# Moving an image's closing pass one image later

## The chip, the cores and the metric

The kernel runs on one core of a Trainium2 chip. The metric is the time of one execution on the device, in microseconds, lower is better; the runs of one kernel are told by their median. The engines are TensorE (PE in the profile; PEld is its weight load), VectorE (DVE), ScalarE (ACT), GpSimd (POOL) and SyncE (SP), which here only issues transfers.

## What is computed

Four images of 96 channels and 128 x 128 pixels pass two layers. Layer 0 is a state-space block; here only its end matters, a norm over channels and a projection whose result, added to the input, is `xnew`. Layer 1 splits the normed image into a positive and a negative half, convolves them, and combines:

```python
xr, x1, x2 = _relu_split_norm(x, sc1, sc2, res_coef, nc1, nc2)
y1 = _layer_norm(_attn_conv(x1, x2, aw1, aw2, aw3))      # od in the kernel
y2 = _layer_norm(_conv2d(x2, w_conv2, K // 2)) * x1      # c2d in the kernel
y = jnp.concatenate([y1, y2], axis=1)
return xr + _conv2d(y, w_full, 0) + b_full[None, :, None, None]
```

`_attn_conv` makes three maps of an image (key, query and value), a softmax over products of the first two, and convolves the value with that softmax as its weights. Both layer norms run over a whole image, so their means and variances exist only when the last row of the image is done. The last line is therefore a pass of its own over the image: the close.

## The kernel before

Up to about 3640 us the scan of layer 0 runs, and beside its end the maps of image 0. What follows is a loop over images `b` (L2598). For each image a foreground, `attention(img, at)` (L1959), works through eleven strips of 12 rows (the last has 8). For images 1 to 3 it makes the maps first: for each strip key and value from `x1p` (m = 0), query and the second convolution from `x2p` (m = 1), on TensorE with weights `wd`, combined on VectorE (`outputs`, L1531). After the last strip stands the softmax (`taps.weights()`, L1683), then the stack of weights `wa` is loaded (`product_stack`, L1367), and the same eleven strips are convolved with them: here called the products. Image 0 has its maps already (`img.mapped`) and only has products here.

The statistics are gathered on the way: `bn_stats` of the second convolution into `c2a` and `c2b`, of the products into `ost` (L2106). Those buffers exist twice, for even and for odd images.

Beside the foreground runs a background, the generator `light`, a chain of:

- `norm` (`ssm_output`, L936): the norm and projection of the next image, mostly on TensorE, which writes `xnew`;
- `split` (`split_norm`): reads `xnew` twice, first for counts, then for the halves `x1p` and `x2p`, with `L1267` on VectorE once for every half plane (64 in an image) and the planes from it on VectorE and GpSimd;
- `close` (`attn_output`, L2299): first the set-up, in which `own_weights` (L2259) and `c2_weights` (L2224) aggregate the statistics (`bn_aggr` at L192 and L2235) and make two weight matrices `w1` and `w2`; then 16 pieces of 1024 pixels. A piece loads `od`, `c2d` and `xnew`, makes `x1` (L2283, L2284), `c2` (L2326) and the residual `e` (L2288 to L2290), multiplies on TensorE (L2334, L2335), adds (L2337 for image 0, L2339 for the others) and stores to `out` (L2341).

`co_run` (L302) interleaves the two at recording: each step of the foreground yields a cost, and the background is advanced by as much. `drain` (L359) records all that is left. Since norm and split of image `b + 1` stand ahead of the close of image `b - 1` in the chain, and `drain(light)` (L2603) stands at the head of images 2 and 3, close 0 is recorded in one piece at the head of image 2, and close 1 beside the products of image 2 with its end at the head of image 3. Image 3 has close 2 (with `share` 2, which counts each piece double and so spreads it), then `before` (L2359), which stores `x1` and `e` of the last image, and after the maps `beside`, which combines the second convolution. What is left of the last image comes after the loop (`after`, L2418).

After recording, a scheduler places the instructions on each engine's queue. It need not keep the recorded order between foreground and background; transfers are issued mostly from SP's queue, in order too.

Of the kernel before, what the change touches and what calls it, by code (L numbers as in the profile page):

```python
# [9 lines left out]
F32 = mybir.dt.float32  # L10
# [7 lines left out]
C = 96  # L18
H = W = 128
L = H * W  # L20
# [51 lines left out]
def kernel(  # L72
# [26 lines left out]
    nc = tc.nc  # L99
# [87 lines left out]
    def combine(ps, stats, mat, name, mv=None):  # L187


        if mv is None:  # L190
            mv = small.tile([stats.shape[0], 2], F32, name="mv", tag=f"mv{stats.shape[0]}")
            nc.vector.bn_aggr(mv, stats)  # L192
        n = mv.shape[0]
        p1 = bank(ps)[:n, 0:2]
        nc.tensor.matmul(p1, lhsT=mat, rhs=mv, start=True, stop=True)  # L195
        r = small.tile([n, 2], F32, name=name, tag=name)
        nc.vector.tensor_copy(r, p1)
        d2 = small.tile([n, 1], F32, name=f"d2{n}", tag=f"d2{n}")
        nc.vector.tensor_sub(d2, mv[:, 0:1], r[:, 0:1])
        nc.vector.tensor_mul(d2, d2, d2)  # L200
        p2 = bank(ps)[:n, 0:2]
        nc.tensor.matmul(p2[:, 0:1], lhsT=mat, rhs=d2, start=True, stop=True)  # L202
        nc.vector.tensor_add(r[:, 1:2], r[:, 1:2], p2[:, 0:1])
        return r, mv
# [154 lines left out]
    def drain(gen):  # L359
        for _ in gen:  # L360
            pass
# [1005 lines left out]
    def product_stack(pool, wd, name, eng=nc.sync):  # L1367


        n = wd.shape[3]  # L1370
        w1 = pool.tile([128, NP, n], F32, name=f"{name}1", tag=f"{name}1")
        w2 = pool.tile([128, NP, n], F32, name=f"{name}2", tag=f"{name}2")
        w3 = pool.tile([128, 2, n], F32, name=f"{name}3", tag=f"{name}3")
        eng.dma_start(w1[0:96], wd[:, 0])
        eng.dma_start(w1[96:128], wd[64:96, 1])
        for h in (1, 2):
            eng.dma_start(w2[64 * h - 64 : 64 * h], wd[0:64, h])
        for j, of in enumerate((FOUR, TWO)):
            for i, p in of:
                eng.dma_start(w3[p : p + 32, j], wd[64:96, 2, i])  # L1380
        return w1, w2, w3
# [577 lines left out]
    def attention(img, at):  # L1959
# [9 lines left out]
        if not img.mapped:  # L1969
# [62 lines left out]
            for s, (r0, r) in enumerate(chunks):  # L2032
# [56 lines left out]
                        yield from taps.some(1 if m else 2)  # L2089
                taps.complete(s, min(r, 3 * NV - r0))  # L2090
            yield from taps.weights()
            ws = product_stack(p1, taps.wt, "wa", nc.scalar)
            img.maps_made()
        else:
            ws = product_stack(p1, img.watd, "wa", nc.scalar)
        yield 3.0
        for i, (r0, r) in enumerate(chunks):
            t, fill, load = at.strip()
            oc = own[0:C, : AR * W]
            here = img.last and r0 >= H - OWN  # L2100
            if here:
                oc = img.last.own[0:C, (r0 - H + OWN) * W :]

            def out(oc=oc, r0=r0, r=r, here=here):
                for a in range(0, r, 4):
                    nc.vector.bn_stats(  # L2106
                        img.ost[:, (r0 + a) // 4], oc[:, a * W : (a + 4) * W]
                    )
                if not here:
                    nc.sync.dma_start(img.od[:, r0 * W : (r0 + r) * W], oc[:, : r * W])  # L2110
                img.finished = r0 + r == H

            v = oc[:, : r * W]
            if img.mapped:
                v = v.rearrange("p (h w) -> p h w", w=W)
            else:
                v = v.rearrange("p (h j t) -> p h j t", j=TW, t=TN)
            to = [(0, C, v)]
            evac = outputs(p2, C, r * TN, to, later, out)
            yield from products(ps, [(0, C, 0, t, 0, r)], ws, later, evac, fill=[  # L2120
                both(fill[0], load[0]), fill[1], both(fill[2], load[1]),
                fill[3], both(fill[4], load[2]), fill[5],
            ])
# [97 lines left out]
            yield from lift(H)  # L2221
            later.flush()

    def c2_weights(img, ps, pool):  # L2224


        n = NSTRIP
        mva, mvb = (pool.tile([128, 2], F32, name=f"mv_{i}") for i in "ab")
        for mv, st, p, e, k in (
            (mva, img.c2a, 96, 128, 4 * n - img.mapped),  # L2230
            (mvb, img.c2b, 0, 64, 2 * n - (not img.mapped)),
            (mvb, img.c2b, 64, 128, 2 * n - 1),
        ):
            v = st[p:e, :k].rearrange("p c s -> p (c s)")
            nc.vector.bn_aggr(mv[p:e], v)  # L2235
        halves = ((mva[96:128], m96[96:128]), (mvb, mrows[img.mapped]))

        def over(n):
            pt = bank(ps)[:, 0:n]
            for i, (mv, mat) in enumerate(halves):  # L2240
                nc.tensor.matmul(
                    pt, lhsT=mat, rhs=mv[:, 0:n], start=(i == 0), stop=(i == 1)
                )
            return pt

        s2 = pool.tile([128, 2], F32, name="s2")
        nc.vector.tensor_copy(s2, over(2))
        for mv, p in ((mva, 96), (mvb, 0)):
            d = mv[p:128, 0:1]
            nc.vector.tensor_sub(d, d, s2[p:128, 0:1])  # L2250
            nc.vector.tensor_mul(d, d, d)
        nc.vector.tensor_add(s2[:, 1:2], s2[:, 1:2], over(1))
        r2 = col("r2")
        rsqrt(r2, s2[0:C, 1:2])
        w2 = pool.tile([C, C], F32, name="w2")
        nc.vector.tensor_scalar(w2, wful[:, 1], r2, None, ALU.mult)
        return s2, w2

    def own_weights(img, ps, pool):  # L2259

        so, _ = combine(ps, img.ost.rearrange("p c s -> p (c s)"), mean96, "so")
        ro = col("ro")
        rsqrt(ro, so[:, 1:2])
        w1 = pool.tile([128, C], F32, name="w1")
        nc.vector.tensor_scalar(w1[0:C], wful[:, 0], ro, None, ALU.mult)
        nso = col("nso")
        nc.vector.tensor_scalar(nso, so[:, 0:1], -1.0, None, ALU.mult)
        pt = bank(ps)[C : C + 1, 0:C]  # L2270
        nc.tensor.matmul(pt, lhsT=img.keep["low"][:, 1:2], rhs=ident, start=True, stop=False)
        nc.tensor.matmul(pt, lhsT=nso, rhs=w1[0:C], start=False, stop=True)  # L2272
        nc.vector.tensor_copy(w1[C : C + 1], pt)
        return w1[0 : C + 1]
# [171 lines left out]
    class Image:  # L2446


        def __init__(self, b):
            self.b = b  # L2450
            self.xnew = dram.tile([C, L], F32, name="xnew", bufs=3)
            self.x1p, self.x2p, self.vp = planes[b % 2]
            self.x1d, self.x2d, self.vd = maps if b == 0 else (None, None, None)
            self.stats = istats[b % 2].tile([C, NCH, 6], F32, name="xstats", tag="xstats")
            self.cnt = istats[b % 2].tile([C, 5, NS], F32, name="cnt", tag="cnt")
            self.keep = {}
            self.mapped, self.lifting = False, False
            self.done = [0, 0]
            self.finished = False
            self.last = None  # L2460
            self.maps_made = lambda: None
            self.watd = None if b else dram.tile([C, 3, NP, C], F32, name="watd", bufs=1)

        def begin(self):

            self.c2d, self.od = (dram.tile([C, L], F32, name=n) for n in ("c2d", "od"))
            n = NSTRIP
            self.c2a, self.c2b, self.ost = (
                istats[self.b % 2].tile([p, k, 6], F32, name=m, tag=m)
                for m, p, k in (("c2a", 128, 4 * n), ("c2b", 128, 2 * n), ("ost", C, H // 4))  # L2470
            )
# [121 lines left out]
    def maps_made(last):  # L2593
        maps_only.close()
        pool = ctx.enter_context(tc.tile_pool(name="e2", bufs=1, side="left"))
        last.kept = pool.tile([C, NS, SN], F32, name="e2")

    for b in range(NB):  # L2598
        after = []
        if b:  # L2600
            if b > 1:
                drain(light)
            imgs[b].begin()  # L2603
            if b + 1 < NB:
                imgs[b + 1] = Image(b + 1)
                after.append(imgs[b + 1].norm(yms[(b + 1) // 2][(b + 1) % 2], psr, "right"))
                after.append(
                    imgs[b + 1].split(psr, "right", lambda i, second: second)
                )
            after.append(imgs[b - 1].close(psr, "right", 1.0 if b + 1 < NB else 2.0))  # L2610
            if b + 1 == NB:
                last = imgs[b].last = LastOutput(imgs[b], psr, "right")
                imgs[b].maps_made = lambda: maps_made(last)
                after += [last.before(), last.beside()]
        light = chain(light, *after)
        left = imgs[b].attend(at)
        co_run(left, light, 1.0 if b else 1.5)
        drain(left)
# [79 lines left out]
```

## Time and profile before

| | us |
|---|---|
| median of 3 runs | 6416.27 |
| lowest, highest | 6413.48, 6428.01 |
| the profiled execution's own time | 6409.68 |
| its span in the profile | 6407.8 |
| mean granted TensorE clock | 0.902 |

| stage (us from the span's start) | foreground | background |
|---|---|---|
| 3826 to 4502 | maps of image 1 | end of split 1, norm 2, split 2 |
| 4502 to 4632 | products of image 1 | end of split 2 |
| 4632 to 5430 | maps of image 2 | close 0, norm 3, split 3 |
| 5430 to 5612 | products of image 2 | most of close 1 |
| 5612 to 6195 | maps of image 3 | end of close 1, close 2, `before` |
| 6195 to 6356 | products of image 3 | `beside` |

The stages of the second table are cut where the first matmul of each stage starts on TensorE; the background is told by the stores of its parts. A row of the profile's view by stretches gives the length of the stretch and then, engine by engine, its busy time and the number of its instructions, the granted clock of TensorE, the mean busy share of the 16 DMA engines and the rate in GB/s. A row of its groups gives the line, the engine, the operation, what it writes and reads, the shapes and the number; then the busy time in us and the mean of one in ns; then the idle time of the engine before them and what ended it. A row of its waits gives who waited for whom, the total in us, the number of times and the longest.

### The profile page before, as it was taken

Reading aid. Unit: us, or ns where it says so; the run is one execution under the profiler, and the core shown is the slowest. Engines: PE = TensorE matmul, PEld = TensorE weight load, DVE = VectorE, ACT = ScalarE, POOL = GpSimd, SP = SyncE. Lnnn points to the kernel's source line nnn. Section 1 sums busy time; section 2 is a strip of 40 time slices with the busy share of each in tenths; the row PEclk is TensorE's granted clock in tenths of the full one; section 3 lists DMA queues with packets and bytes.
Section 4 is the critical chain, followed back from the end, with each engine's and each line's share of the span. In section 5 each row is a group of like instructions: output and inputs, shape, how many; then the busy total and the mean of one; then the engine's idle time right before and its main releaser. Section 6 shows DMA issues by size and latency. Waiting matters only on the chain. (4 is left out here: it accounts for less than half of the span.)

```text
span 6407.8 us, 76468 instructions
## 1 busy us (share of the span) xinstructions
PE 5253.4 (82%) x23264; PEld 2254.8 (35%) x23264; DVE 4699.9 (73%) x7132; ACT 3759.4 (59%) x4770; POOL 3238.6 (51%) x2476
## 2 busy tenths in 40 slices
PE   6889988987888643989988588977888877889888
PEld 2333322322222111444433234345333444345553
DVE  4247878988989768989844686468774687988767
ACT  1247767787787666777622465466644665545642
POOL 1326757978879554979822234436304365022310
PEclk9899989998999765999999799989989888999989
DMA  6766777775675766676667686665776656967668
GB/s 155 175 160 189 198 199 199 214 221 163 198 202 171 202 183 207 196 213 179 182 185 195 166 228 163 195 169 156 214 199 184 175 149 165 245 167 180 191 168 221
DMA packets 897706, 1205.30 MB, mean 188 GB/s; under 512 B 230644, under 2 KB 745642, under 8 KB 884816
## 3 DMA queue, kind: packets, MB, share of 16 engines
q1 hardware_dynamic: 866640, 1145.36, 65.5%
q0 software_dynamic: 16336, 38.51, 2.3%
q10 hardware_dynamic: 14320, 16.54, 0.9%
q8 instruction: 187, 3.06, 0.2%
q14 instruction: 223, 1.83, 0.1%
HBM read 777.82 MB, written 345.62 MB: 175 GB/s over the span
## 5 line engine op out<-in xcount | busy, mean ns | idle before, releaser
L633 PE MATMUL bank<-y,wp 128*128 128x512 f32 (+3 forms) x3584 | 1310.9, 622 | 83.8 <-DMA y<-y 41.0
L866 POOL TENSOR_TENSOR y<-y,dl 128x1024 f32<-128x1024 f32 x384 | 1058.5, 2757 | 263.0 <-DVE dl L858 240.3
L833 POOL TENSOR_TENSOR dl<-dl,u 128x1024 f32<-128x1024 f32 x384 | 1008.8, 2627 | 253.1 <-ACT dA L809 121.1
L854 DVE TENSOR_TENSOR_SCAN dA<-dA,pBC 128x512 f32<-128x512 f32 x768 | 981.6, 1278 | 30.7
L2169 PE MATMUL bank<-y,wn 128*64 128x384 f32 (+5 forms) x2408 | 680.1, 507 | 58.3 <-DMA y<-x1d 34.1
L1477 PE MATMUL two<-ya,wd 128*64 128x192 f32 (+3 forms) x2376 | 582.2, 414 | 174.0 <-ACT odd L1550 65.1
L633 PEld LDWEIGHTS bank<-y,wp 128*128 128x128 f32 (+3 forms) x3584 | 456.2, 168 | 749.3 <-issue 651.1
L858 DVE TENSOR_TENSOR dl<-dA,pBC 128x512 f32<-128x512 f32 x768 | 528.5, 688 | 255.8 <-PE pBC L747 183.8
L747 PE MATMUL pBC<-xr,wbc 60*128 60x512 bf16 (+1 forms) x1536 | 457.8, 404 | 311.5 <-DVE dA L854 239.1
L1938 ACT COPY yb<-ya 64x768 f32<-64x768 f32 (+1 forms) x660 | 537.7, 815 | 195.5 <-PE two L1477 113.8
L676 ACT ACTIVATE dl<-pd,dtb 128x512 f32<-128x512 f32 x768 | 485.5, 684 | 187.9 <-PE pd L747 171.5
L1477 PE MATMUL two<-yb,wd 128*64 128x192 f32 (+3 forms) x2376 | 559.0, 400 | 4.0 <-ACT yb L1938 4.0
L837 DVE TENSOR_TENSOR pBC<-dl,pBC 128x512 f32<-128x512 f32 x768 | 527.5, 687 | 8.8 <-POOL dl L833 7.8
L2169 PEld LDWEIGHTS bank<-y,wn 128*64 128x64 f32 (+3 forms) x2408 | 310.3, 169 | 357.2 <-issue 186.2
L809 ACT ACTIVATE dA<-dl,negA 128x1024 f32<-128x1024 f32 x384 | 420.3, 1141 | 2.3
L1477 PEld LDWEIGHTS two<-ya,wd 128*64 128x64 f32 (+1 forms) x2376 | 262.2, 165 | 370.9 <-ACT odd L1550 75.0
L676 ACT ACT_TABLE_LOAD x248 | 318.2, 1283 | 91.9 <-PE pd L747 79.7
L747 PEld LDWEIGHTS <-wbc 60*128 60x128 bf16 (+1 forms) x1536 | 103.1, 96 | 752.1 <-issue 739.3
L1477 PEld LDWEIGHTS two<-yb,wd 128*64 128x64 f32 (+1 forms) x2376 | 289.7, 167 | 150.5 <-issue 42.1
L1477 PE MATMUL two<-ya,wa 128*96 128x384 f32 (+1 forms) x528 | 231.2, 521 | 72.9 <-DMA ya<-vp 27.0
L1550 ACT COPY odd<-two 128x384 f32<-128x384 f32 (+5 forms) x176 | 115.8, 658 | 291.3 <-PE two L1492 179.1
L1406 POOL TENSOR_TENSOR pl<-x 96x256 f32<-96x256 f32 (+3 forms) x396 | 275.2, 710 | 0.0
(322 smaller groups left out, 9105.4 us busy)
## 6 DMA issues: line engine op xcount, KB each, us to landing
u<-zb SPq DMA_DIRECT2D x192, 1024.0 KB
yms<-y SPq DMA_DIRECT2D x96, 512.0 KB
xn<-xnew SPq DMA_DIRECT2D x128, 384.0 KB
ya<-vp SPq DMA_DIRECT2D x120, 336.0 KB
y<-y SPq DMA_DIRECT2D x128, 258.2 KB
zb<-z SPq DMA_DIRECT2D x64, 512.0 KB
y<-yms SPq DMA_DIRECT2D x64, 512.0 KB
ya<-x1p SPq DMA_DIRECT2D x90, 336.0 KB
```

The source lines that it names most:

```text
L633: nc.tensor.matmul(blocks(pz[p:e]), lhsT=ws[k][:, d, c : c + e - p], rhs=window(ys[k], at, d, n), start=(i == 0), stop=(i == len(terms) - 1),)
L676: nc.scalar.activation(dst, src, AF.Softplus, bias=bias)
L747: nc.tensor.matmul(p, lhsT=w[rows], rhs=xr[rows, at : at + CH], start=True, stop=True)
L809: nc.scalar.activation(live[m]["dA"], live[m]["dl"], AF.Exp, scale=negA[:, g % 3, k : k + 1])
L833: nc.gpsimd.tensor_mul(t, t, u_view(n))
L837: nc.vector.tensor_mul(p, live[n]["dl"][:, bass.ts(half, CH)], p)
L854: nc.vector.tensor_tensor_scan(h, h, p, init, ALU.mult, ALU.add)
L858: nc.vector.tensor_mul(live[n]["dl"][:, sl], live[n]["dA"][:, sl], live[n]["C", half])
L866: nc.gpsimd.tensor_add(v, v, t.rearrange("p (a b) -> p a b", b=W))
L1477: nc.tensor.matmul(of(to[p:e], r), lhsT=w[:, i, c : c + e - p], rhs=tiles(t[k][PAIR[i]][:, SLOT[i]], o, r), start=(k == 0), stop=False,)
L1938: nc.scalar.copy(yb[k][64 * h - 64 : 64 * h, :, :n], ya[k][0:64, :, h * TN : h * TN + n])
L2169: nc.tensor.matmul(pc[p:e, :n].rearrange("p (h w) -> p h w", w=W), lhsT=w[:, c : c + e - p], rhs=v[:, :, 0:W], start=(i == 0), stop=(i == ...
```

## The change

A close runs one image later. Image 1's background is then norm 2 and split 2 alone; image 2's is close 0, norm 3, split 3, with the close first; image 3's is close 1, close 2, `before` and `beside`, all closes with `share` 1. The `drain(light)` at the head of images 2 and 3 is gone.

Since an image's buffers of statistics are written again two images later, a new function `c2_totals` makes means and variances as soon as the image's maps are done, before its product weights are loaded, and `out` does so for `ost` with the last strip. They are kept in `mvs`, six columns in the pool `small`, which keeps two. In DRAM, `xnew` gets a fourth buffer, `c2d` and `od` a third.

```diff
             yield from taps.weights()
+            c2_totals(img)
             ws = product_stack(p1, taps.wt, "wa", nc.scalar)
             img.maps_made()
         else:
+            c2_totals(img)
             ws = product_stack(p1, img.watd, "wa", nc.scalar)
...
-                img.finished = r0 + r == H
+                if r0 + r == H:
+                    nc.vector.bn_aggr(img.mvs[0:C, 4:6], img.ost.rearrange("p c s -> p (c s)"))
+                    img.finished = True
...
-    def c2_weights(img, ps, pool):
+    def c2_totals(img):
         n = NSTRIP
-        mva, mvb = (pool.tile([128, 2], F32, name=f"mv_{i}") for i in "ab")
+        img.mvs = small.tile([128, 6], F32, name="mvs", tag="mvs")
+        mva, mvb = img.mvs[:, 0:2], img.mvs[:, 2:4]
         for mv, st, p, e, k in (
...
             nc.vector.bn_aggr(mv[p:e], v)
+
+    def c2_weights(img, ps, pool):
+        mva, mvb = img.mvs[:, 0:2], img.mvs[:, 2:4]
...
-        so, _ = combine(ps, img.ost.rearrange("p c s -> p (c s)"), mean96, "so")
+        so, _ = combine(ps, None, mean96, "so", img.mvs[0:C, 4:6])
...
-            self.xnew = dram.tile([C, L], F32, name="xnew", bufs=3)
+            self.xnew = dram.tile([C, L], F32, name="xnew", bufs=4)
...
-            self.c2d, self.od = (dram.tile([C, L], F32, name=n) for n in ("c2d", "od"))
+            self.c2d, self.od = (dram.tile([C, L], F32, name=n, bufs=3) for n in ("c2d", "od"))
...
+    closes = {NB - 2: (0,), NB - 1: range(1, NB - 1)}
     for b in range(NB):
         after = []
         if b:
-            if b > 1:
-                drain(light)
             imgs[b].begin()
+            after += [imgs[i].close(psr, "right", 1.0) for i in closes.get(b, ())]
             if b + 1 < NB:
                 imgs[b + 1] = Image(b + 1)
                 after.append(imgs[b + 1].norm(yms[(b + 1) // 2][(b + 1) % 2], psr, "right"))
...
-            after.append(imgs[b - 1].close(psr, "right", 1.0 if b + 1 < NB else 2.0))
```

## Prediction

> **What bounds the kernel now.** I read the page first, then cut the second half of the run into stretches, then asked which instructions fill the stretches that the change touches, then divided the last maps by strip. The page's first part gives averages:
>
> ```profile
> PE 5253.4 (82%) x23264; PEld 2254.8 (35%) x23264; DVE 4699.9 (73%) x7132; ACT 3759.4 (59%) x4770; POOL 3238.6 (51%) x2476
> ```
>
> Two engines stand high and neither is full; the page's chain breaks off after 1% and covers only the last microseconds. So the answer must come by stretch. The stage of image 1 is 3826 to 4632, that of image 2 4632 to 5612, that of image 3 5612 to 6356. The cuts are where strips of maps begin on TensorE (eleven strips of 12 rows to an image).
>
> ```profile
> core 0: us, PE busy (x) PEld busy (x) DVE busy (x) ACT busy (x) POOL busy (x), PEclk, DMA share, GB/s
> 3826.00:3976.00 150.00, 127.27 (x832) 71.19 (x832) 108.66 (x201) 80.35 (x110) 70.08 (x107) 0.91 0.59 156
> 3976.00:4222.00 246.00, 216.38 (x1211) 93.92 (x1212) 120.07 (x265) 112.79 (x159) 100.45 (x132) 0.97 0.67 186
> 4222.00:4502.00 280.00, 211.70 (x1493) 137.20 (x1491) 225.68 (x469) 190.69 (x281) 152.93 (x227) 0.86 0.61 160
> 4502.00:4632.00 130.00, 117.98 (x412) 50.74 (x412) 107.75 (x207) 83.75 (x110) 40.78 (x58) 0.96 0.81 222
> 4632.00:4777.00 145.00, 117.17 (x349) 44.34 (x346) 113.72 (x130) 56.34 (x57) 13.71 (x13) 0.84 0.73 203
> 4777.00:5029.00 252.00, 227.62 (x1251) 95.15 (x1250) 120.49 (x266) 116.82 (x164) 99.26 (x133) 0.96 0.67 188
> 5029.00:5095.00 66.00, 46.20 (x296) 27.88 (x295) 42.92 (x94) 47.73 (x78) 11.45 (x20) 0.82 0.67 171
> 5095.00:5430.00 335.00, 256.87 (x1790) 167.97 (x1788) 278.40 (x555) 200.84 (x284) 205.56 (x295) 0.84 0.58 151
> 5430.00:5612.00 182.00, 164.53 (x502) 67.07 (x502) 153.94 (x198) 93.64 (x109) 5.70 (x16) 0.95 0.90 241
> 5612.00:5916.00 304.00, 273.34 (x1536) 145.30 (x1537) 249.64 (x363) 144.70 (x178) 82.10 (x102) 0.95 0.68 176
> 5916.00:6195.00 279.00, 236.58 (x1779) 154.46 (x1777) 196.67 (x344) 156.97 (x202) 84.24 (x137) 0.92 0.66 179
> 6195.00:6356.00 161.00, 148.72 (x466) 62.08 (x466) 120.86 (x177) 64.82 (x82) 5.41 (x6) 0.93 0.84 219
> ```
>
> In the rows of 3976 and 4777 a norm runs beside maps: TensorE near 90%, VectorE under 50%. In the rows of 4222 and 5095 a split does: VectorE 81 and 83%. The first strip of image 2 (4632 to 4777) holds all of close 0, the products of image 2 (5430 to 5612) hold 13 of the 16 pieces of close 1, and the first five strips of image 3 hold its other 3 and close 2. VectorE is at 78 to 85% there. Compare the two rows of products, 4502 and 5430: the same matmuls take 130 us beside a bit of a split and 182 beside a close.
>
> What a piece of a close (1024 pixels) costs, from VectorE's groups between 4632 and 6356:
>
> ```profile
> L2284 DVE SCALAR_TENSOR_TENSOR x<-xx,kept,x 96x1024 f32<-96x1024 f32 x64 | 84.3, 1317 | 50.4 <-ACT x L2283 34.4 <-DMA od<-own 12.8 <-DMA out<-x 2.7
> L2339 DVE TENSOR_TENSOR x<-bank,e 96x512 f32<-96x512 f32 x64 | 64.8, 1036 | 21.5 <-PE bank L2335 20.9
> L2337 DVE TENSOR_TENSOR x<-bank,e 96x512 f32<-96x512 f32 x32 | 21.5, 683 | 9.9 <-PE bank L2335 9.6
> ```
>
> Four such passes (median 1.275 each, L2284, L2289, L2290, L2326) and two additions: 4 x 1.275 + 2 x 1.036 = 7.2 us of VectorE, for image 0 with L2337 6.5. TensorE has four matmuls, eight records of 0.59 (3.4 us of streaming), ScalarE two passes of 1.23, SP three loads and a store of 393 KB each. What a piece costs in time shows where strips of the last maps carry different numbers. Records of L2334, four to a piece, in strips 1 to 4:
>
> ```profile
> 5679.00:5751.00 72.00, 11.88 (x24) 3.35 (x24) 0.95 0.72 189
> 5751.00:5805.00 54.00, 5.96 (x12) 1.72 (x12) 0.97 0.76 194
> 5805.00:5869.00 64.00, 7.99 (x16) 2.28 (x16) 0.97 0.64 158
> 5869.00:5916.00 47.00, 3.93 (x8) 1.31 (x8) 1.00 0.72 189
> ```
>
> 6, 3, 4 and 2 pieces take 72, 54, 64 and 47 us. The best line is 36 + 6.3 per piece. From two pieces on, a piece costs about its VectorE time. The last two strips, with nothing beside them, take 45 and 56: below two pieces it costs little.
>
> [...] But the change puts closes (VectorE) beside bare maps, not beside the norm, which would have VectorE to spare; the norm keeps its strips to itself. [...] image 2's exponentials end on ScalarE by 5410.2, but VectorE's reciprocal of their sum (L1701) runs at 5414.88, behind the 16 small instructions of close 1's set-up that stand before it. Hence I count what stands ahead of what in the built order.
>
> **The change, part by part.** The profiled execution took 6409.7 us (span 6407.8), 6.6 under the median of 6416.3; the sums are made against the first.
>
> Where things stand comes from the order of the built kernel. Nothing moves up to the end of image 0's direct maps, and image 1's stage is the same but for three aggregates. Image 2: the 16 pieces of close 0 stand in strips 0, 1, 2 (3, 7, 6 on TensorE) instead of all in strip 0; the norm moves from strips 1 to 3 to strips 3 to 5; the split's half-plane instructions (L1267) from strips 5 to 10 to strips 7 to 10, with 20 of 64 from the end of the maps on. Close 1 leaves the products. Image 3: its strips get 0.5, 7, 7, 7, 8, 2.5 pieces, where they had about 4, 6, 3, 4, 2 and none; `before` (L2366) follows behind, as before at four pieces a strip. The products of image 3 and the end keep theirs.
>
> Image 2, maps, now 798 us (4632 to 5430). Strip 0: the burst gives 145 = 41.5 + 16 x 6.5, so 41.5 + 3 x 6.5 = 61. Strips 1 and 2: 36 + 7 x 6 = 78 and 36 + 6 x 6 = 72. The other eight strips carry norm and split just as image 1's last eight do, 246 + 280 = 526; image 2's own norm rows are a little longer, so 530. Sum 741: 57 less. In this is also the softmax without close 1's set-up in front (3 to 4 us).
>
> Image 2, products, now 182. Image 1's took 130 with 15 half-plane instructions; here there are 20, each with its share of the planes about 2.5 us of VectorE, so 12 us on an engine 83% busy. 137: 45 less. DMA, at 0.90 now, falls to the 0.81 of image 1.
>
> Image 3, maps, now 583. Strips 1 to 4, now 237 us, with 7, 7, 7, 8 pieces over the line's 36: at 6.3 each (the line) 327, at 7.2 (VectorE's time) 353. I take 6.7 and 338, so 101 more. Strip 0 loses its pieces of close 1 on TensorE, but VectorE does three ahead: 50 for 67. Strip 5, 2.5 pieces and `before`: 51 for 47. Strips 6 to 10: 4 more for `before` standing one piece later. Sum 92 more. The moved pieces' 13 x 1.57 = 20 MB spread over some 390 us, so DMA goes from 176 to about 190 GB/s, under what the products bear (241).
>
> Image 0's transition (3640 to 3682): the aggregates (L2235, 1.34 and 0.71) now stand before the softmax's maximum, with VectorE without a gap; TensorE waits 27 us here. Three loads of `wa` on ScalarE's queue now stand behind two copies that wait for `vp`. Together 2 to 4 us, against about 1 that the lifted planes win by going ahead: 2 more. At the ends of maps 1 to 3 the aggregate of `c2a` lies in a gap of VectorE, waiting for TensorE (2.4 us at 4478): nothing; without that gap 1.3 each. The aggregate of `ost` only changes its place. The third and fourth DRAM buffers cost no instruction; `mvs` has two buffers, and image 2 wants the first back some 500 us after close 0 has read it. The `drain` removed has nothing left to drain after image 1.
>
> Sum: -57 - 45 + 92 + 2 = -8 us. The change moves VectorE's work and removes none; what it gains is the place where a close costs most (the products, 182 - 137), and it pays nearly as much in the last maps.
>
> **The rivals.** A: the trade above, nearly even: 6408 (own range 6388 to 6428, from 10 us either way in each of the two large sums).
> B, slower: crowded closes cost more than their VectorE time. Place: strips 1 to 4 of image 3, 29 pieces. SP issues in order, and a store that waits for VectorE holds back the `ya` loads behind it; in the stages shown it did so 11 times:
>
> ```profile
> SPq L2341 <- DVE x L2339: 61.9, 11, 9.6
> ```
>
> Also each piece needs the two banks of the piece before. For: VectorE was busy only 78% in the burst and 82% beside close 2. Strips 1 to 4 hold 29 x 7.2 us of closes and 4 x 22 of their own (a bare strip's VectorE rows), 297 us; at 0.80 that is 371, 33 more than I took: +25, 6441. Against: the products had the same chain at 85%. The trade turns negative from 7.0 us a piece, and shows from 7.4.
> C, faster: the pieces cost 6.3, image 2 takes image 1's 526 and 130: -8 - 11 - 4 - 7 = -30, or -45 if the first strips overlap better too: 6371 to 6386. For: VectorE at 45 to 55% in the bare strips. Against: `before` takes those strips.
> D: the change doesn't do what it says, because the scheduler puts the closes back. The built order excludes it.
>
> **How the numbers follow.** A 0.50, B 0.29, C 0.20, D 0.01. I predict A's 6408. The range: A's and C's and B's centres with the ends of the strips' price, 6368 to 6446. A measurement of this kernel can tell about 0.2% (13 us) from no change. A is faster than that in a third of its width and seldom slower; with C faster 0.37, with B slower 0.30, 0.33 between.
>
> **What would show it.** Right: the products of image 2 in 132 to 142 us; image 2's maps in 730 to 755; strips 1 to 4 of image 3 at 80 to 90 each with VectorE at 85% or more, 29 pieces in them; image 1 unchanged in its 806. Wrong: strips at 95 and over, with TensorE waiting for `ya` or L2339 (B); last maps under 650 (C); image 2's products still above 160, which would mean that it was not the close that held them; or a change in image 1's stage, which my account leaves out.

## The result and the profile after

The change makes the kernel slightly slower. Its median is 6428.91 us over 18 runs, that of the kernel before in the same comparison 6413.48 over 18; the ratio is 1.0023, 95% interval 1.0012 to 1.0033, so 8 to 21 us. The prediction said 6408, 8 us less than before. The profiled execution has a span of 6418.8 us and a mean granted clock of 0.899 (0.902 before).

Line numbers after the constructor of the statistics are 9 higher than before: `first_half` is L2292 and L2293, `residual` L2297 to L2299, the close's product and additions L2335, L2343 to L2348, its store L2350, `before`'s load L2375 and stores L2389. The first line of the page, set beside the one shown before:

```profile
PE 5294.5 (82%) x23264; PEld 2269.0 (35%) x23264; DVE 4686.4 (73%) x7132; ACT 3765.8 (59%) x4770; POOL 3232.3 (50%) x2476
```

The same number of instructions, and VectorE's busy time even falls by 13.5 us; TensorE's rises by 41. The view by stretches shows where, cut at the same first matmuls as before (first image 2's norm, its split, its products; then the first five strips of image 3's maps, the other six, its products):

```profile
core 0: us, PE busy (x) PEld busy (x) DVE busy (x) ACT busy (x) POOL busy (x), PEclk, DMA share, GB/s
4817.00:5085.00 268.00, 240.46 (x1241) 99.88 (x1242) 116.29 (x257) 115.16 (x163) 97.63 (x132) 0.92 0.63 174
5085.00:5373.00 288.00, 216.76 (x1504) 139.79 (x1502) 231.34 (x471) 188.00 (x277) 150.02 (x221) 0.85 0.60 157
5373.00:5510.00 137.00, 121.68 (x411) 51.89 (x412) 107.40 (x201) 87.33 (x113) 46.42 (x67) 0.93 0.79 220
5510.00:5893.00 383.00, 339.26 (x1623) 165.84 (x1624) 313.51 (x434) 167.36 (x195) 70.74 (x101) 0.91 0.69 183
5893.00:6211.00 318.00, 264.82 (x1797) 165.31 (x1795) 213.17 (x358) 165.71 (x210) 84.76 (x138) 0.89 0.64 174
```

By stage, from the two traces:

| stage | before | forecast | after |
|---|---|---|---|
| maps of image 1 and its products | 806 | 806 | 809 |
| maps of image 2 | 798 | 741 | 754 |
| products of image 2 | 182 | 137 | 137 |
| maps of image 3 | 583 | 675 | 701 |
| of these, strips 1 to 4 | 237 | 338 | 345 |
| of these, strips 5 to 8 (they hold `before`) | 178 | not told apart | 221 |

The maps of image 1, which of all versions only the very last one touches, took between 669 and 680 us in the 19 other traces; a difference of a few us between two traces shows nothing by itself.

Strips 1 to 4 came out near the forecast, in the records of the matmul L2343 with 7, 7, 7 and 8 pieces:

```profile
5548.00:5621.00 73.00, 13.96 (x28) 3.67 (x28) 1.00 0.69 187
5621.00:5708.00 87.00, 16.49 (x28) 4.73 (x28) 0.91 0.70 187
5708.00:5795.00 87.00, 16.66 (x28) 4.92 (x28) 0.88 0.69 185
5795.00:5893.00 98.00, 18.57 (x32) 5.83 (x32) 0.86 0.66 172
```

They do lose clock from strip to strip (third number from the end: 1.00, 0.91, 0.88, 0.86). The larger surprise lies behind them. Strips 5 to 8 of the kernel before, then of the kernel after:

```profile
5916.00:6094.00 178.00, 155.75 (x1155) 98.75 (x1154) 140.88 (x220) 110.04 (x134) 58.09 (x84) 0.95 0.69 193
```

```profile
5893.00:6113.00 220.00, 184.23 (x1170) 108.63 (x1169) 159.62 (x235) 120.46 (x144) 57.61 (x83) 0.90 0.67 188
```

Nearly the same work (15 matmuls and 15 VectorE instructions more, the last two to three pieces of close 2), 42 us more. No engine is full (TensorE, the busiest, 184 of 220 us); the granted clock is lower, 0.90 for 0.95.

### The profile page after: what moved, and what is told of

Its sections match the earlier page's. It is cut to its first block, busy times and chain, and to the rows that moved or that the text cites. A ratio compares the mean times of both kernels' runs of the same rounds, so it can differ in the third digit from the quotient of the medians.

```text
span 6418.8 us, 76472 instructions
## 1 busy us (share of the span) xinstructions
PE 5294.5 (82%) x23264; PEld 2269.0 (35%) x23264; DVE 4686.4 (73%) x7132; ACT 3765.8 (59%) x4770; POOL 3232.3 (50%) x2476
## 5 line engine op out<-in xcount | busy, mean ns | idle before, releaser
L1477 PE MATMUL two<-ya,wd 128*64 128x192 f32 (+3 forms) x2376 | 594.0, 419 | 140.7 <-ACT odd L1550 49.1
L1477 PE MATMUL two<-yb,wd 128*64 128x192 f32 (+3 forms) x2376 | 567.8, 403 | 13.3 <-ACT yb L1938 13.3
L1477 PEld LDWEIGHTS two<-ya,wd 128*64 128x64 f32 (+1 forms) x2376 | 268.3, 167 | 342.4 <-issue 92.9
L1477 PEld LDWEIGHTS two<-yb,wd 128*64 128x64 f32 (+1 forms) x2376 | 296.7, 168 | 167.3 <-issue 50.0
L1550 ACT COPY ends<-two 128x384 f32<-128x384 f32 (+5 forms) x176 | 116.2, 661 | 291.3 <-PE two L1492 284.0
L1477 PE MATMUL two<-ya,wa 128*96 128x384 f32 (+1 forms) x528 | 229.5, 518 | 66.7 <-DMA ya<-vp 29.2
```

The costliest lines, as they stand in the source:

```text
L1477: nc.tensor.matmul(of(to[p:e], r), lhsT=w[:, i, c : c + e - p], rhs=tiles(t[k][PAIR[i]][:, SLOT[i]], o, r), start=(k == 0), stop=False,)
```

## The experiments

All ratios are to the kernel before, run beside it on the same chip. Times of strips and stages come from one trace of each version; they are cut at first matmuls as above. "Maps 3" is image 3's maps. A bare strip, one with nothing beside it, takes 40 us (strips 7 to 9 of the version with the statistics and share 1, below: 40.4, 40.0, 39.9).

**First, the parts and the price of a close.**

The statistics alone: the changed kernel with the loop of the kernel before.

```diff
-    closes = {NB - 2: (0,), NB - 1: range(1, NB - 1)}
...
+            if b > 1:
+                drain(light)
...
-            after += [imgs[i].close(psr, "right", 1.0) for i in closes.get(b, ())]
...
+            after.append(imgs[b - 1].close(psr, "right", 1.0 if b + 1 < NB else 2.0))
```

> The statistics part of the change alone (c2_totals, mvs, the DRAM buffers); closes, chain and drains as before. Theory 1 (the closes' new place costs it: crowded in the last maps): within 3 us of the kernel before, so 6410 to 6417. Rival (the aggregates in front of the softmax, or what they do to the order, cost it): most of the +15 us shows here, 6425 or more.

Measured: 6388.20, ratio 0.9976 (0.9967 to 0.9986): 15 us faster, which neither expectation had. Maps 3 take 568 us instead of 583, 8.5 of the 15 in strip 0. There, in the kernel before, TensorE waits for VectorE inside close 2's set-up; with the aggregates made earlier that wait is not there. The waits of TensorE in strip 0, before:

```profile
PE bank L202 <- DVE d L200: 1.9, 1, 1.9
```

After that gap (5653.9) the granted clock of the kernel before is 0.50 from 5656.3 for 10.24 us; over the strip it is 0.87, with the statistics alone 0.97. In these 10.24 us two matmuls of L1477 (128x384) take 1.5 to 1.65 us, where they took 0.81 just before, so they do the work of about 5. If the half speed is put down to the gap, the wait of 1.9 us came to about 2 + 5, most of the 8.5; that is the author's estimate. The rest of the 15 is spread and not explained here.

Close 1 left out, once of each kernel:

```diff
-            after.append(imgs[b - 1].close(...))
+            if b != 2:
+                after.append(imgs[b - 1].close(...))
```

> The kernel before without the close of image 1, which is left out and whose output is not written: its price where it stood. Theory 1: products of image 2 fall from 182 to 125 to 135 us, the first strip of image 3 from 67 to about 45, in all 65 to 80 us less, about 6340. Rival (a close costs its VectorE time wherever it stands, some 115 us): 6300.

```diff
-    closes = {NB - 2: (0,), NB - 1: range(1, NB - 1)}
+    closes = {NB - 2: (0,), NB - 1: (NB - 2,)}
```

> The changed kernel without the close of image 1, left out in the same way: its price in the crowded maps. Theory 1: the maps of image 3 fall from 701 to 560 to 590 us, so close 1 costs 110 to 140 here, about 6300, and the kernel is then faster than the kernel before without close 1. Rival (same price in both places, and the loss comes from norm and split of image 3 having been put back): 6340 to 6360, not faster than the other.

Measured: 0.9834 (0.9815 to 0.9853) and 0.9872 (0.9858 to 0.9887): close 1 costs 106 us where it was (1.66%) and 97 where it went (1.0023 - 0.9872 = 1.51%), each known to about 12 us, so the two prices are not told apart. The first is near its rival's 115, over the 65 to 80 of theory 1; the second is under its 110 to 140. Crowding close 1 is therefore not what made the kernel slower: without it the changed kernel is still the slower one, by 24 us (0.9872 against 0.9834). Where that stays can be seen in maps 3: 548 against 598 us for the same work, 16 pieces and `before`.

The closes of image 3 spread as the last one was before (`share` 2):

```diff
-            after += [imgs[i].close(psr, "right", 1.0) ...]
+            after += [imgs[i].close(psr, "right", 2.0 if b + 1 == NB else 1.0) ...]
```

> The changed kernel with the two closes of image 3 counted double, so that they stand at four pieces a strip over eight strips instead of seven or eight over four, and `before` behind them. Theory 1 (the price of a piece grows with their number in a strip, the first two are nearly free): strips 1 to 8 at 58 to 64 us, the maps of image 3 at 620 to 640 instead of 701, some of it given back by `before` beside the last strips and the products: 6375 to 6400. Rival (VectorE's total decides, and it is as full at four as at seven): 6420 to 6430.

Measured: 6450.74, ratio 1.0068 (1.0055 to 1.0081). Maps 3 fall to 651, with four pieces a strip at about 61 us, but the closes now reach into strip 8, half of `before`'s tiles and all of `beside` are pushed past the maps, and products 3 with the end take 277 instead of 208.

**Then, why `before` is dear.** In strips 5 to 8 ScalarE waits for loads of `xnew`, in the kernel before and in the changed one:

```profile
ACT x L2283 <- DMA xx<-xnew: 1.9, 1, 1.9
```

```profile
ACT x L2292 <- DMA xx<-xnew: 14.8, 5, 6.4
```

Loads further ahead:

```diff
-                    y = p3.tile([C, SN], F32, name="xx")
+                    y = p3.tile([C, SN], F32, name="xx", bufs=3)
...
-                ahead = load(0)
+                ahead = [load(0), load(1)]
...
-                        ahead = load(t + 1)
+                        ahead.append(load(t + 2))
```

> The changed kernel, with a third buffer for `xx` in `before` of the last image, so that each load of `xnew` is issued two tiles ahead instead of one; nothing else differs. So far strips 5 to 8 of image 3's maps, which carry `before`, took 221 us here and 178 in the kernel before, with the same instructions; the trace has ScalarE waiting 14.8 us for `xnew` there (1.9 before), and what it copies out of TensorE's banks stands behind that wait. Theory L (the loads come late, because SP holds them behind stores): ScalarE's wait for `xnew` in these strips falls under 3 us, the four strips to 185 to 200, the run 20 to 35 us under the changed kernel, so 6395 to 6410 or a ratio to the kernel before of 0.997 to 1.000. Theory P (it is where `before`'s passes stand within a strip's order, ahead of the copies that TensorE waits for): the wait for `xnew` goes, but the strips stay at 212 or more and the run within 10 us of the changed kernel, ratio 1.001 to 1.003.

Measured: strips 5 to 8 220 us (221), ratio 1.0031 (1.0014 to 1.0048). Early loads alone don't help: ScalarE's wait for `xnew` falls to 8.1, and 8.5 us of waiting for the stores of `x1s` to free their buffers take its place.

One empty step ahead of `before`, half a tile, and later a quarter:

```diff
+                yield 4.6        # 2.3 in the second
                 ahead = load(0)
```

> The changed kernel, with `before` begun half a tile later: one more empty step of cost 4.6 ahead of its first tile, which shifts all 16 tiles by about an eighth of a strip in the order of emission; no instruction is added or taken away. Theory P (the place of the passes within a strip): strips 5 to 8 change by 15 us or more, most likely down from 221 towards 178 to 200, the run 20 to 40 us under the changed kernel. Theory L (late loads): 210 to 225 as before, the run within 8 us of the changed kernel, ratio 1.001 to 1.003. A third account, that crowded closes ahead leave something late that `before` inherits, expects no change either.

> The changed kernel with the empty step ahead of `before` at 2.3 instead of 4.6, a quarter of a tile: the shift by half a tile put ScalarE's passes nearly where the other half of a tile had stood and changed nothing (222 us for strips 5 to 8). If the place of the passes within a strip decides: 175 to 205. If not: 215 to 225.

Measured: strips 5 to 8 222 us, ratio 1.0031 (1.0013 to 1.0048), and 213 us (one run). Neither comes near 178.

`before` first, the closes behind it:

```diff
+            run = [imgs[i].close(psr, "right", 1.0) for i in closes.get(b, ())]
...
-            after += [imgs[i].close(psr, "right", 1.0) for i in closes.get(b, ())]
...
-                after += [last.before(), last.beside()]
+                after += [last.before(), *run, last.beside()]
```

> The changed kernel, with the order of the last image's beside-work turned round: `before` of image 3 in strips 0 to 4, then the closes of images 1 and 2 in strips 5 to 9 (about 8, 7, 8, 6, 3 pieces). Same instructions. If `before` is dear only behind the closes (theories P and L, since neither its place in a strip nor what SP holds is the same here): its strips at 43 to 50 as in the kernel before, strips 5 to 9 at 80 to 95, maps of image 3 650 to 675 instead of 701, the run 25 to 50 us under the changed kernel, ratio 0.995 to 0.999. If every 16 tiles of `before` cost 44 us more at share 1 whatever precedes: 695 to 710 and no gain. If the closes pay more at the maps' end: strips 5 to 9 over 100 and the run slower than the changed kernel.

Measured: 6443.83, ratio 1.0051 (1.0031 to 1.0072). Strips 1 to 4, which hold 15 of `before`'s 16 tiles, take 201 us: dear with no close in front of it as well. And the closes in strips 5 to 8 take 366.

A third schedule, close 1 at the end of image 2's chain at pace 1.15:

```diff
-    closes = {NB - 2: (0,), NB - 1: range(1, NB - 1)}
+    closes = {NB - 2: (0,), NB - 1: (NB - 2,)}
...
+            if b + 2 == NB:
+                after.append(imgs[b - 1].close(psr, "right", 1.0))
...
-        co_run(left, light, 1.0 if b else 1.5)
+        co_run(left, light, (1.5, 1.0, 1.15, 1.0)[b])
```

> A third schedule: the changed kernel with close 1 put behind image 2's split instead of into image 3 and image 2's beside-work paced at 1.15, so that some 2 pieces of close 1 lie in the end of image 2's maps and most of the others in its products; close 2 alone is in image 3. From the stages measured so far: image 2's maps 750 to 770 (754 in the changed kernel), its products 165 to 182 (137 and 182), image 3's maps about 600 (598 without close 1). Sum against the kernel before: -40 in maps 2, -5 to -15 in products 2, +10 to +20 in maps 3, and -10 from the statistics: 6365 to 6385, ratio 0.993 to 0.997. If a burst of close pieces in the products costs more than in the kernel before (over 182), or image 3's maps take over 620, it is no better than 0.998.

Measured: ratio 1.0032 (1.0022 to 1.0042), a miss: the faster pace crowds image 2's norm strips (125 and 98 us against 105 and 79), maps 2 take 793.

**Share.** The change also lowers the last close's share from 2 to 1. Share 1.3 for all of image 3's closes, and share 1 with the closes left where they were:

```diff
-            after += [imgs[i].close(psr, "right", 1.0) ...]
+            after += [imgs[i].close(psr, "right", 1.3 if b + 1 == NB else 1.0) ...]
```

> The changed kernel with the closes of image 3's stage at share 1.3 instead of 1.0: about 5.3 pieces a strip instead of 7, so that they reach into strip 6 and `before` follows in strips 6 to 10. From the strips measured so far, over a bare strip of 41 us: pieces cost 4.1 to 4.7 us each where there are 3 to 6 to a strip (the kernel before, alone and without close 1), 5.9 where there are 7 or 8 (the changed kernel). Theory D (a piece's price rises with the number in a strip[...]): 32 pieces at 4.6 to 5.2, `before` 16 to 55 us over bare, maps of image 3 625 to 670 instead of 701, the run 6365 to 6400, ratio 0.993 to 0.998. Theory V (a piece costs its VectorE time whatever the density, and `before` behind closes is dear): maps of image 3 690 to 705 and the run within 10 us of the changed kernel, ratio 1.001 to 1.003.

```diff
-            after.append(imgs[b - 1].close(psr, "right", 1.0 if b + 1 < NB else 2.0))
+            after.append(imgs[b - 1].close(psr, "right", 1.0))
```

> The kernel with the statistics part alone (each close where the kernel before has it), with the last close at share 1 instead of 2, which is one more thing that the change does: the 3 left pieces of close 1 and close 2 lie 4, 8 and 7 in strips 0 to 2 of image 3, `before` in strips 3 to 6. With share 2 its maps of image 3 took 568 us, four strips with `before` 175. If share 1 makes pieces and `before` dearer by itself: strips 1 and 2 at 85 to 95, the strips with `before` alone at 53 to 58 each, maps of image 3 600 to 625, the run 30 to 50 us slower than with share 2, ratio 1.002 to 1.005. If the strips with `before` are dear only where closes were moved between images: 43 to 48 each, maps of image 3 565 to 585, ratio 0.997 to 1.000.

Measured: 1.0003 (0.9995 to 1.0011) with maps 3 at 681, and 1.0050 (1.0035 to 1.0065) with maps 3 at 610. The second, set against the statistics alone, is the cleanest pair of the study: same statistics, same closes in the same images, and share 1 alone takes 42 us more in maps 3 than share 2. It also gives the price of the move itself: maps 2, products 2 and maps 3 together take 1593 us with the closes where they were and 1592 in the changed kernel; by the runs the move gains 17 us. So the 15 us of the whole change are a sum of three: the statistics -15, share +47 (0.9976 to 1.0050), the move -17 (1.0050 to 1.0023); share is measured with the closes unmoved, and the last two are known to about 12 us each.

Of the 42 us 33 lie in the four strips with `before`, here at share 2 (the statistics alone) and then at share 1:

```profile
5900.00:6075.00 175.00, 153.21 (x1158) 97.08 (x1156) 140.77 (x221) 110.34 (x134) 57.08 (x84) 0.97 0.70 196
```

```profile
5830.00:6038.00 208.00, 172.58 (x1152) 104.23 (x1153) 143.18 (x230) 114.19 (x138) 55.46 (x87) 0.90 0.64 182
```

What SP waited for in the same two windows, share 2:

```profile
SPq L1450 <- POOL sm L2025: 13.2, 1, 13.2
...
SPq L1450 <- POOL pl L1406: 4.6, 1, 4.6
```

and share 1:

```profile
SPq L1450 <- POOL pl L1406: 34.9, 2, 18.7
```

In the changed kernel's strips 5 to 8:

```profile
SPq L1450 <- POOL pl L1406: 15.0, 1, 15.0
SPq L1450 <- POOL sm L2025: 14.3, 1, 14.3
```

L1450 stores the value planes `vp`, which GpSimd sums; SP reaches the store early and stands there: 17.8 us at share 2, 34.9 at share 1, 29.3 in the changed kernel (19.1 in the kernel before), and 27.2 in the four strips of the version with `before` first. What stands behind it, in the time order of SP's queue at share 1:

```profile
5887.10 0.31 SPq L2389 DMA_DIRECT2D es<-e  x1
5906.20 2.54 SPq L1450 DMA_DIRECT2D vp<-pl  x4
5908.84 0.55 SPq L2375 DMA_DIRECT2D xx<-xnew  x1
5909.43 0.91 SPq L2030 DMA_DIRECT2D c2d<-sm  x2
5910.38 0.94 SPq L1913 DMA_DIRECT2D ya<-x2p  x2
```

From 5887.4 to 5906.2 SP issues nothing. Behind the hold stand `before`'s load and the `ya` loads of TensorE's next matmuls; TensorE's waits in this window have

```profile
PE two L1477 <- DMA ya<-x2p: 3.9, 1, 3.9
```

a gap from 5911.8 on. At share 2 the load of `xnew` stands ahead of the hold, which is short there:

```profile
5950.30 0.69 SPq L2375 DMA_DIRECT2D xx<-xnew  x1
5955.71 2.54 SPq L1450 DMA_DIRECT2D vp<-pl  x4
```

This is one place, worth 3.9 us of the 33 by the wait itself; the granted clock, 0.97 over the four strips at share 2 and 0.90 at share 1, was not divided by place. To test the account as a whole, take the stores that wait off SP's queue. First `before`'s own, on top of the loads two ahead:

```diff
                     for d, y in ((self.x1d, x1), (self.ed, e)):
-                        nc.sync.dma_start(d[:, bass.ts(t, SN)], y)
+                        nc.gpsimd.dma_start(d[:, bass.ts(t, SN)], y)
```

> The changed kernel with three buffers for `xx`, loads two tiles ahead, and `before`'s 32 stores (`x1s`, `es`) issued by GpSimd instead of SP, so that nothing of `before` that waits for VectorE stands in SP's queue ahead of `ya` loads. Strips 5 to 8 took 220 us with the loads alone moved ahead. If SP's in-order queue is what makes them dear: 180 to 200. If it is the order of the passes on VectorE and ScalarE: 212 to 228. If GpSimd's own planes are held up by the stores: over 230.

Measured (one run): strips 5 to 8 206 us, maps 3 685 against 699 with the loads alone: part of it, and short of the range expected of SP's queue. Then the stores that hold, in image 3 only:

```diff
                             store_planes(
-                                nc.sync, img.vp[c0:c1], at, n,
+                                nc.gpsimd if img.last else nc.sync, img.vp[c0:c1], at, n,
```

on the changed kernel,

> The changed kernel with one difference: in image 3's maps the stores of value planes (`vp` from `pl`, line L1450 as the values call it) are issued by GpSimd, which makes the planes, instead of SP, so that SP no longer waits for GpSimd's sums ahead of `before`'s transfers and the `ya` loads. Theory S (SP's in-order queue, held by these stores, is what makes `before` dear behind closes at share 1): strips 5 to 8 from 221 to 185 to 200, maps of image 3 from 701 to 660 to 680, ratio 0.997 to 1.000. Theory O (the order of passes on VectorE and ScalarE): strips 5 to 8 at 212 or more, maps of image 3 at 690 or more, ratio 1.001 to 1.003. If issuing costs GpSimd more than the wait cost SP, it is slower: over 705.

on the statistics alone,

> The kernel with the statistics part alone (share 2, closes where the kernel before has them), with the same stores of `vp` on GpSimd. It has 568 us for image 3's maps and 175 for strips 5 to 8, 14 over bare strips, so there is little to win: theory S expects 555 to 570 and a ratio of 0.995 to 0.998, theory O 565 to 572 and 0.997 to 0.999.

on share 1.3,

> The changed kernel with share 1.3 in image 3 and the stores of `vp` on GpSimd. With share 1.3 alone image 3's maps took 681 and the ratio was 1.0003; about 40 us of that lay in strips 7 to 10, which carry `before`. Theory S: 640 to 660, ratio 0.994 to 0.998, the best of all if at the low end. Theory O: 675 to 685, ratio 0.999 to 1.001.

and on share 1 with the closes where they were:

> The kernel with the statistics part and share 1 for the last close (closes not moved; 1.0050, image 3's maps 609.5, its strips 3 to 6 with `before` 208 us), with the `vp` stores of image 3's maps on GpSimd. Theory S (share 1 costs because `before` then stands behind SP's hold): strips with `before` 185 to 195, maps of image 3 575 to 595, ratio 0.998 to 1.001. If share 1 is dear for another reason (the closes' density): 600 to 612, ratio 1.003 to 1.005.

| kernel | ratio without | ratio with `vp` off SP | maps 3 | four strips with `before` (tiles of it) |
|---|---|---|---|---|
| changed | 1.0023 | 0.9974 (0.9964 to 0.9984) | 701, 668 | 221 (16, and 3 pieces), 198 (16) |
| statistics alone, share 2 | 0.9976 | 0.9988 (0.9976 to 0.9999) | 568, 579 | 175 (16), 186 (14) |
| share 1.3 | 1.0003 | 0.9977 (0.9967 to 0.9986) | 681, 657 | not cut |
| statistics, share 1 | 1.0050 | 1.0009 (0.9998 to 1.0020) | 610, 592 | 208 (16), 182 (14) |

With that one queue changed the changed kernel goes from slower than the kernel before to faster, 31 us in all; strips 1 to 8 of image 3 fall from 566 to 532. At share 1 with the closes unmoved about half of what share had cost comes back. Where share is 2 nothing is gained: the intervals overlap, and maps 3 take 11 us more. With `vp` off SP the move of the closes is a gain of 22 us by itself (1.0009 to 0.9974).

But in the changed kernel the gain is mostly not in `before`. Its strips fall by 23 us, and three pieces of close 2, worth 19 at 6.4 each, have left them: over bare strips the 16 tiles cost about 42 us and then still 38. The closes are what became cheaper: strips 1 to 4 take 334 for 32 pieces where they took 345 for 29, so a piece costs 5.4 us over a bare strip where it cost 6.4. SP's largest waits in strips 5 to 8 with `vp` off its queue:

```profile
SPq L1921 <- PE two L1492: 62.0, 8, 12.5
SPq L2030 <- POOL sm L2025: 18.0, 9, 5.1
```

L1450 is gone, and SP is now held by TensorE freeing buffers, that is, it runs ahead of its readers. `before`'s loads are not earlier for it: ScalarE still waits 14.3 us for `xnew` in these strips, and at share 2 the same edit raises that wait from 2.7 to 14.4. Taking stores off a queue also lets the scheduler set close pieces otherwise (8, 8, 9 and 7 in strips 1 to 4 of the changed kernel; 10 in strip 1 of the table's last row, which took 110 us), so no pair of these differs in the queue alone, and how much of a gain is due to the new order is open. SP's largest wait in maps 3 of the changed kernel, 142 us of the closes' stores (L2350) for VectorE, was left as it is; what it holds up was not tested.

Last, the other stores that wait for GpSimd, `c2d` from `sm` (L2030), together with `vp` and with share 1.3; in image 3, as shown, and then both in all images:

```diff
-                nc.sync.dma_start(img.c2d[64:96, at : at + n * W], t[:, : n * W])
+                (nc.gpsimd if img.last else nc.sync).dma_start(img.c2d[64:96, at : at + n * W], t[:, : n * W])
```

> Share 1.3, the closes moved, and in image 3's maps both kinds of stores that GpSimd's results wait for (`vp` from `pl` and `c2d` from `sm`) on GpSimd; with `vp` alone it was 656.5 us for these maps and 0.9977. SP was held 55 us by `sm` in such maps. If that hold costs like the other: 640 to 650, ratio 0.994 to 0.997. If `sm` comes early enough for nobody to wait, or GpSimd's time to issue 44 more stores takes it back: 652 to 662, ratio 0.997 to 0.999.

> As the run before it, but in the maps of images 1 and 2 too, where SP is held 42 and 47 us by `sm` and part of 53 and 33 by planes. If the hold costs there too: maps of images 1 and 2 at 655 to 668 and 725 to 742 (671 and 749 now), ratio 0.990 to 0.994. If those stages are bound by VectorE's split and the norm: within 5 us of now, ratio as in the run before it. GpSimd is busier there (split's sums), so that it could also lose: maps over 680 and 755.

Measured: 6368.01, ratio 0.9931 (0.9906 to 0.9956, four runs), maps 3 at 642 and its strips 6 to 9 at 44 to 47: the best version, 44 us under the kernel before. In all images 1.0004 (0.9996 to 1.0013), a miss: maps 1 go from 677 to 735 and maps 2 from 750 to 767, of which shorter products give back 21 and 15. In maps 1 issuing the 87 stores takes GpSimd 48 us (0.5 to 0.6 each), and SP now waits for GpSimd's sum in the norm (L1045), whose result it stores as `xnew`; first with the stores moved in image 3 only, then in all:

```profile
SPq L1098 <- POOL r L1045: 4.9, 3, 3.9
```

```profile
SPq L1098 <- POOL r L1045: 72.8, 11, 13.2
```

## Why the prediction was wrong, point by point

Right were the products of image 2 (137.2 for 137), image 1 unchanged (809 for 806), and the trade of rival A, that closes moved into the last maps cost about what they cost before: 97 against 106 us for close 1, not told apart, and 1 to 17 us gained by the move at equal share (traces, runs).

Two terms of the sum failed: the last maps, put at +92 us and measured at +118, where `before` was taken to cost the same behind denser closes and the change of share was not priced; and the statistics, put at nothing and measured at -15.

Maps 3 took 701 us for 675: strip 0 12 less than forecast (38 for 50), strips 1 to 4 7 more, strip 5 8 more, and strips 6 to 10, the term "4 more for `before`", took 260 where they had taken 232, 24 more than forecast. The working took `before` to cost the same wherever it stands, since it has the same instructions at the same four tiles a strip; it counted SP's waits only for the closes. The runs show another price: 15 us over four bare strips at share 2, 48 at share 1, about 42 in the changed kernel. And the step folded the change of share into the count of pieces per strip. Share was an edit of its own, and the largest: +42 us of maps 3 with all else equal, 33 of them in the strips with `before`. Why share 1 costs so much is shown in part: about half comes back when GpSimd's planes are stored from another queue (22 us over bare strips then, for 14 of the 16 tiles). In the changed kernel 38 us stay, so what else makes `before` dear there is open, and so is the part of the closes; crowding is a candidate (10 pieces in one strip took 110 us).

That strips 1 to 4 came to 345 for 338 is partly luck. The line behind it starts at 36 us, and a bare strip takes 40. The sign set for it, VectorE at 85% or more, did not come: it was busy 94, 81, 79 and 79%, 285 us in all, less than the 297 that rival B's sum counts, at nearly the 0.80 that B gave. A piece's price is not VectorE's time either: with `vp` off SP's queue it fell from 6.4 to 5.4 over a bare strip, under the 7.2 of its VectorE passes. Rival B had the sign of the result, and a hold on SP's queue may have cost something in the closes' strips (the 6.4 and 5.4), but these strips did not reach 371, and TensorE's largest wait in them was for VectorE's `c2` (L2335, 25.8 us), not for `ya` or the additions.

"Statistics at nothing" was wrong by 15 in the other direction. The instructions were costed and not the wait that they cause on TensorE in close 2's set-up, nor the clock after it (0.87 in strip 0, 0.97 with the aggregates made earlier); by the estimate above these are about half of it. That gain lies in maps 3 as well: without it they would have been 41 too long, about the price of share (42).

Image 2's maps were 13 too low (754 for 741): norm strips 268 and split strips 288, together 26 over the 530 taken from image 1's rows of 246 and 280. Strip 0 was cheaper (47 for 61).

The term of 2 us at image 0's transition could not be seen: its products took 144 us before, 139 after, 141 to 146 in the other kernels. Over the stages of the sum the traces give -44 - 45 + 118 - 5 = +24 where -8 was forecast. The two spans differ by 11, since the scan ended 11 us earlier in this one profile (3671 against 3682, 3670 to 3690 over all kernels), image 1 took 2 us more and the end 5 less; the medians differ by 15.

## What to carry to other kernels

List a queue's waits by what stands behind each, not only by their length: in image 3 a store that waits for GpSimd cost nothing visible at share 2 and about half of 42 us at share 1, with other loads behind it. When a change moves work and its pacing at once, cost the pacing as an edit of its own. Here a store that waited for the engine that makes its data was issued from that engine instead, and SP's waits at it, 29.3 us in strips 5 to 8 of the changed kernel, were gone; that paid in image 3 (1.0023 to 0.9974). With both kinds of stores moved, images 1 and 2, where GpSimd also had the norm and the split to serve, cost again what image 3 had won (0.9931 in image 3 alone, 1.0004 in all). The freed queue ran on to its next wait (62.0 us for L1492), and the loads behind did not come notably earlier: ScalarE waited 14.3 us for `xnew` after 14.8.

## What the hardware showed beside that

Some short waits of TensorE were followed by half speed that cost more than the wait. The clock record of the changed kernel has two values, 1.0 and 0.5. In the kernel before, one record of the close's matmuls (L2334, L2335) starts a median 0.43 us after the one ahead of it at 1.0, and 0.85 us at 0.5. Stretches at 0.5 in the changed kernel come in whole multiples of 3.41 us (141 of 142; 61 are of one, 45 of two, 17 of three), and in strips 5 to 8 each begins within 4 us of the start of a TensorE gap of 1.4 us or more; two gaps of 1.7 us were followed by none. Over all of image 3's maps 17 of 19 stretches begin so, and 17 of 25 such gaps are followed by one; in the kernel before it is 10 of 18, with the statistics alone 4 of 17, so a gap of this length does not suffice, and what decides was not found. Gaps of 1.9 us (strip 0 before) and 3.3 us (at 5969 after) were each followed by 10.24 us at 0.5, with no further gap of 0.25 us or more in these; how long such a stretch lasts did not follow from the gap's length here, for a gap of 3.4 us (at 6029 after) was followed by 3.41 us. In maps 3 the time at 0.5 grew from 75 us to 137; half of the difference, an estimate from the 0.43 and 0.85 us above, is 31 of the 118 us that these maps grew.
